# Inverse row transform by even and odd frequencies, issued in a hand-written order

## The chip, the cores and the metric

The kernel runs on one core of a Trainium2 chip. The core has a matrix engine (TensorE, PE in the profile), a vector engine (VectorE, DVE), a scalar engine (ScalarE, ACT), GpSimd (POOL) and a queue engine that only issues transfers (SyncE, SP). Times are device microseconds of one execution; a kernel's time is the median of several runs.

## What is computed

The input x has shape 16 x 16 x 256 x 256 (batch b, channel, row y, column x). Two layers follow, each of the form "add to x what a block makes of the group norm of x":

```python
# layer 0: a Laplace operator with learned poles, in the frequency domain
alpha = fft2(gn(x))
output_residue1 = einsum('biox,oxik->bkox', alpha, S)        # steady part
x1 = ifft2(output_residue1).real
x2 = einsum('kbiqz,biqx->kizx', F, E2).real                  # transient part, from the poles
x = x + x1 + x2 / Nx / Ny
# layer 1: convolutions, mish and a channel gate, on gn(x)
x = x + _L1_conv_ref(gn(x), ...)
```

gn is a group norm with 8 groups of 2 channels. Since x1 is real, the transform back needs only half of the row frequencies, 128 of them with a real and an imaginary part. The change concerns the last steps of layer 0: the inverse transform along the rows (over y), the sum with x2 and with x, the mean and variance of the result, and its normalized copy for layer 1.

## The kernel before

The program has four parts, one after the other, that hand tensors on through device memory: layer0_forward (forward transforms, pole sums, and tables that are computed in small pieces between its steps), layer0_mix (the mixing of channels and the inverse transform along the columns), layer0_back (the inverse transform along the rows and the norm) and layer1. All arithmetic is fp32.

*layer0_mix* writes hd. Its function columns (line 680 on) makes, for each row frequency fy and each half q of the batch, a tile o of 128 partitions (8 batches x 16 channels) with a real and an imaginary row of 256 columns, by a copy of the odd half on ACT (line 701) and two additions on DVE (704 and 705). One transfer per tile, issued by POOL (line 709), stores it; the real frequencies 0 and 128 share a row, so they are stored by line 715. hd has the shape frequency, batch, channel, part v, column.

*layer0_back* loops over 16 batches and, in each, over four groups of four channels: 64 groups and 256 channels. Per group it loads h (four channels of hd, 128 frequencies in the partitions, 1 MB, line 815) and x (four channels, 1 MB, line 820). For every second channel a matmul of 512 columns (828) makes pf, the pole part for two channels, which ACT copies to f (832). For each channel py gets two row halves yh, and each half takes three matmuls of 256 columns: the cosine and the sine frequencies (837, v = 0 and 1, stationary operand a slice of iy) and the pole part (840, f against e2). DVE adds py into x (843) and takes the statistics of the sum (844). After four channels two aggregates (847) follow, then group_norm_scalars (lines 30 to 54), a generator that is run to its end at once: a matmul with a matrix of 1/128 for the mean over partitions (34), small DVE operations (36 to 39), a second such matmul for the variance (42), and eight small operations of DVE with a square root on ACT (44 to 53). Last, z = (x - mean) / std is written by DVE for two channels and by POOL for the other two (854), and two transfers store it to zn (863).

The instruction order of TensorE, ACT, DVE and POOL in layer0_mix and layer1 is written out by hand (manual_schedule), and in layer0_forward that of TensorE alone. In layer0_back a scheduler of the compiler sets it. SP's order, that is the order of loads and of the stores to zn, is the scheduler's everywhere. A tile pool gives each named tile a number of buffers (bufs); a writer waits until the reader of the buffer's last content is done.

Of the kernel before, what the change touches and what calls it, by code (L numbers as in the profile page):

```python
# [10 lines left out]
F32 = mybir.dt.float32  # L11
I32 = mybir.dt.int32
AF = mybir.ActivationFunctionType
ALU = mybir.AluOpType
AX = mybir.AxisListType
PSUM = bass.MemoryType.PSUM
DRAM = bass.MemoryType.DRAM

C = 16
N = 256  # L20
G = 8
P = 128
# [34 lines left out]
def load(nc, pool, src, shape, name):  # L57
    t = pool.tile(shape, F32, tag=name, name=name)
    nc.sync.dma_start(out=t, in_=src)
    return t  # L60
# [322 lines left out]
def tables(ctx, tc, d, psum, tabs):  # L383

    nc = tc.nc
    td, avd, ed = tabs
    cp = ctx.enter_context(tc.tile_pool(name="tc", bufs=1))
# [23 lines left out]
    for k in range(C):  # L411
        e = tp.tile([P, N], F32, tag="te", name="te")
# [22 lines left out]
        for h, wt in enumerate(wts):  # L435
            for part, rhs in ((0, br), (1, e)):
                nc.tensor.matmul(
                    ps[:, h],
                    lhsT=wt[:, part].rearrange("p c i m -> p (c i m)"),
                    rhs=rhs,  # L440
                    start=part == 0,
                    stop=part == 1,
# [59 lines left out]
    for i, axis in enumerate("12"):  # L502
        pr = cp.tile([P, C], F32, name=f"epr{axis}")
        pi = cp.tile([P, C], F32, name=f"epi{axis}")
        for a in range(2):
            nc.sync.dma_start(out=pr[64 * a : 64 * a + 64], in_=d[f"p{axis}r_kp"])
            nc.sync.dma_start(out=pi[64 * a : 64 * a + 64], in_=d[f"p{axis}i_kp"])
        tr = cp.tile([P, N], F32, name=f"etr{axis}")
        nc.sync.dma_start(out=tr, in_=d["ty" if axis == "1" else "tx"].to_broadcast([P, N]))
        for k in range(0, C, 2):  # L510
            arg = tp.tile([P, 2, N], F32, tag="arg", name="arg")
            n = tp.tile([P, 2, N], F32, tag="n", name="n")
            nf, af = n.rearrange("p k x -> p (k x)"), arg.rearrange("p k x -> p (k x)")
            for j in range(2):
                nc.vector.tensor_scalar(arg[:, j], tr, pi[:, k + j : k + j + 1], None, ALU.mult)

            nc.vector.tensor_scalar(n, arg, 1.0 / TWO_PI, phase, ALU.mult, ALU.add)
            nc.vector.tensor_scalar(n, n, ROUND, ROUND, ALU.add, ALU.subtract)
            nc.vector.scalar_tensor_tensor(af, nf, -c1, af, ALU.mult, ALU.add)
            nc.vector.scalar_tensor_tensor(af, nf, -c2, af, ALU.mult, ALU.add)  # L520
            nc.vector.tensor_scalar(arg, arg, turn, None, ALU.add)
            nc.vector.tensor_scalar(arg, arg, 3.1415925, -3.1415925, ALU.min, ALU.max)
            nc.scalar.activation(n, arg, AF.Sin)
            for j in range(2):
                nc.vector.tensor_scalar(arg[:, j], tr, pr[:, k + j : k + j + 1], None, ALU.mult)
            exponential(nc, tp, af)
            if axis == "2":
                nc.vector.tensor_scalar(n, n, last, None, ALU.mult)
            nc.vector.tensor_tensor(arg, arg, n, ALU.mult)
            nc.sync.dma_start(out=ed[:, i, k : k + 2], in_=arg)  # L530
            yield

# [15 lines left out]
def layer0_mix(ctx, tc, d, al, hd, tabs):  # L548
# [133 lines left out]
    def columns(g, f, yt):  # L682
# [16 lines left out]
        for q in range(2):  # L699
            odd = hp.tile([P, 2, P], F32, tag="odd", name="odd", bufs=2)  # L700
            nc.scalar.copy(odd, ph[q][:, 1].rearrange("p (v x) -> p v x", v=2))
            o = hp.tile([P, 2, 2, P], F32, tag="h", name="h", bufs=5)
            even = ph[q][:, 0].rearrange("p (v x) -> p v x", v=2)
            nc.vector.tensor_tensor(o[:, :, 0], even, odd, ALU.add)
            nc.vector.tensor_tensor(o[:, :, 1], even, odd, ALU.subtract)  # L705
            o = o.rearrange("p v h x -> p v (h x)")
            fy = 4 * g + f
            if fy % P:
                nc.gpsimd.dma_start(  # L709
                    out=hd[fy, q:nb:2].rearrange("b k v x -> b (k v x)"),  # L710
                    in_=o.rearrange("p v x -> p (v x)"),
                )
            else:
                part = fy // P
                nc.gpsimd.dma_start(out=hd[0, q:nb:2, :, part], in_=o[:, 0])

    E = mybir.EngineType
    with tc.manual_schedule(engines={E.PE, E.Activation, E.DVE, E.Pool}):
# [60 lines left out]
def layer0_back(ctx, tc, d, hd, bd, zn, mr, ed):  # L779


    nc = tc.nc
    nb = d["x"].shape[0]
    cp = ctx.enter_context(tc.tile_pool(name="bc", bufs=1))
    iy = load(nc, cp, d["iy"], [P, 2, N], "iy")
    ones = load(nc, cp, d["ones"], [P, P], "ones")

    e1 = cp.tile([P, C, N], F32, name="e1")
    e2 = cp.tile([P, C, N], F32, name="e2")
# [1 line left out]
        for i, t in enumerate((e1, e2)):  # L791
            nc.sync.dma_start(out=t[:, k : k + 4], in_=ed[:, i, k : k + 4])

    hp = ctx.enter_context(tc.tile_pool(name="bh", bufs=3))
    fp = ctx.enter_context(tc.tile_pool(name="bf", bufs=3))
    sm = ctx.enter_context(tc.tile_pool(name="bs", bufs=2))
    psf = ctx.enter_context(tc.tile_pool(name="psf", bufs=2, space=PSUM))
    psy = ctx.enter_context(tc.tile_pool(name="psy", bufs=3, space=PSUM))
    psn = ctx.enter_context(tc.tile_pool(name="psn", bufs=1, space=PSUM))

    zero = cp.tile([nb, C * (N + 2)], F32, name="zero")
# [5 lines left out]
        for x in (0, N + 1):  # L807
            nc.gpsimd.memset(t[:, :, :, x : x + 1], 0.0)

    for b in range(nb):  # L810
        r2 = fp.tile([P, P], F32, tag="r2", name="r2")
        nc.sync.dma_start(out=r2, in_=bd[b])
        for k0 in range(0, C, 4):
            h = hp.tile([P, 4, 2, N], F32, tag="h", name="h")
            nc.sync.dma_start(
                out=h.rearrange("p k v x -> p k (v x)"),
                in_=hd[:, b, k0 : k0 + 4].rearrange("f k v x -> f k (v x)"),
            )
            x = hp.tile([P, 4, 2, N], F32, tag="x", name="x")
            nc.sync.dma_start(  # L820
                out=x.rearrange("p k h x -> p (k h) x"),
                in_=d["x"][b, k0 : k0 + 4].rearrange("k (h p) x -> p (k h) x", p=P),
            )
            st = sm.tile([P, 4, 6], F32, tag="st", name="st")
            for k in range(4):
                if k % 2 == 0:
                    pf = psf.tile([P, 2, N], F32, tag="pf", name="pf")
                    nc.tensor.matmul(  # L828
                        pf, lhsT=r2, rhs=e1[:, k0 + k : k0 + k + 2], start=True, stop=True
                    )  # L830
                    f = fp.tile([P, 2, N], F32, tag="f", name="f")
                    nc.scalar.copy(f, pf)
                py = psy.tile([P, 2, N], F32, tag="py", name="py")
                for yh in range(2):
                    ys = slice(P * yh, P * yh + P)
                    for v in range(2):
                        nc.tensor.matmul(  # L837
                            py[:, yh], lhsT=iy[:, v, ys], rhs=h[:, k, v], start=v == 0, stop=False
                        )
                    nc.tensor.matmul(  # L840
                        py[:, yh], lhsT=f[:, k % 2, ys], rhs=e2[:, k0 + k], start=False, stop=True
                    )
                nc.vector.tensor_tensor(x[:, k], py, x[:, k], ALU.add)
                nc.vector.bn_stats(st[:, k], x[:, k].rearrange("p h x -> p (h x)"))
            mv = sm.tile([P, 2, 2], F32, tag="mv", name="mv")
            for g in range(2):
                nc.vector.bn_aggr(mv[:, g], st[:, 2 * g : 2 * g + 2].rearrange("p c s -> p (c s)"))
            g0 = k0 // 2
            nm, rs = mr[:, b, g0 : g0 + 2, 0], mr[:, b, g0 : g0 + 2, 1]
            for _ in group_norm_scalars(nc, sm, psn, ones, mv, 2, nm, rs):  # L850
                pass
            z = zbuf[(4 * b + g0 // 2) % 3]
            for g, eng in ((0, nc.vector), (1, nc.gpsimd)):
                eng.tensor_scalar(
                    z[:, :, 2 * g : 2 * g + 2, 1 : N + 1],
                    x[:, 2 * g : 2 * g + 2].rearrange("p k h x -> p h k x"),
                    nm[:, g : g + 1],
                    rs[:, g : g + 1],
                    ALU.add,
                    ALU.mult,  # L860
                )
            for h in range(2):
                nc.sync.dma_start(
                    out=zn[b, 1 + P * h : 1 + P * h + P, k0 : k0 + 4].rearrange("p k x -> p (k x)"),
                    in_=z[:, h].rearrange("p k x -> p (k x)"),
                )

# [435 lines left out]
def fourier_tables():  # L1305
# [33 lines left out]
    for t in tt:  # L1339
# [5 lines left out]
        "wxa": parities(wx[..., :P]),  # L1345
        "wxn": wxn,
        "ix": ix,
        "iy": iy,
        "ones": np.full((P, P), 1.0 / P),
        "pair": np.stack([np.tile(np.eye(64), (2, 1)), -np.tile(np.eye(64), (2, 1))], axis=1),  # L1350
        "gc": np.tile(np.repeat(np.eye(G), 2, axis=0), (8, 1)),
# [8 lines left out]
        "m8": np.tile(np.repeat(np.eye(8), M, axis=0), (4, 1)),  # L1360
        "mt": mt.reshape(P, 2, 16),
        "phase": np.repeat([0.25, 0.0], 64)[:, None],
        "last": np.repeat([1.0, -1.0], 64)[:, None] / (N * N),
    }
    return {name: a.astype(np.float32) for name, a in out.items()}

# [25 lines left out]
def forward(ctx, tc, d):  # L1392
# [2 lines left out]
    keep = ctx.enter_context(tc.tile_pool(name="keep", bufs=1))  # L1395
    al = dram.tile([NF, 2, 64, nb, N], F32, name="al")
    bd = dram.tile([nb, P, P], F32, name="bd")
    hd = dram.tile([P, nb, C, 2, N], F32, name="hd")
    tabs = (
        dram.tile([P, 2, C, N], F32, name="td"),  # L1400
        dram.tile([NF, P, 384], F32, name="avd"),
# [34 lines left out]
```

## Time and profile before

The time is 7599.57 us, the median of three runs (7587.35 to 7604.02). The profiled execution took 7581.6 us.

| part, as the trace bounds it | us from the start | PE busy | DVE busy | ACT busy | POOL busy |
|---|---|---|---|---|---|
| forward, main stretch | 0 to 1300 | 1192.5 | 1073.3 | 399.8 | 528.3 |
| mix, main stretch | 1500 to 2970 | 1344.5 | 987.8 | 908.6 | 191.0 |
| back, middle 200 us | 3240 to 3440 | 199.4 | 123.5 | 21.2 | 27.7 |
| layer 1 | from 3842 | the rest of the span | | | |

The back part begins with its first row matmul at 2990.2 us and ends with the last z at 3821.8 us; layer 1's first convolution starts at 3842 us.

How to read the lines below. A group of instructions has its source line, engine and operation, output and inputs with shapes and count; behind the first bar stand its total busy time in microseconds and the mean of one in nanoseconds, and behind the second the idle time of the engine just before it, with what ended that wait. A timeline line has its start and its length in microseconds first. The chain of waits is followed back from the last instruction of a stretch: at each step to what released it, or to the instruction before it on its engine. The trace shows an fp32 matmul as two instructions.

### The profile page before, as it was taken

The numbers are of one execution on the slowest core, as the hardware profiler recorded it, in microseconds if no ns is written. First come the engines' busy times: TensorE is split into PE (matmuls) and PEld (weight loads), VectorE is DVE, ScalarE is ACT, GpSimd is POOL, SyncE is SP. The second block draws the span as 40 slices with busy tenths as digits, with TensorE's granted clock in tenths as the row PEclk, the third lists the DMA queues.
The fourth block names the chain that finished last, engine by engine and source line by source line (L and its number), as shares of the span: only waits on it lengthen the run. The fifth ranks groups of instructions, "written<-read, shape, count | busy, mean of one in ns | idle before, by whom it ended". The sixth has DMA issues, their size and how long they took to land.

```text
span 7581.6 us, 148237 instructions
## 1 busy us (share of the span) xinstructions
PE 7060.1 (93%) x58664; PEld 4076.6 (54%) x58664; DVE 4908.4 (65%) x9169; ACT 3712.2 (49%) x5659; POOL 3029.4 (40%) x4126
## 2 busy tenths in 40 slices
PE   7889999799999998999979999999999999999997
PEld 5778888566667666777733333333333333333332
DVE  8999875366666665666656666666666666666662
ACT  2223333366666664111146666666666665666662
POOL 2334444211111111111135555656555666555664
PEclk9999999899999999999989999999999999999999
DMA  3444444333333335767657788888888888888886
GB/s 97 113 115 119 119 118 111 108 97 100 100 95 96 97 97 162 251 243 250 241 151 215 228 255 254 251 265 264 244 252 256 248 267 256 249 254 254 247 266 212
DMA packets 702807, 1443.62 MB, mean 190 GB/s; under 512 B 93866, under 2 KB 520038, under 8 KB 652166
## 3 DMA queue, kind: packets, MB, share of 16 engines
q1 hardware_dynamic: 557990, 959.89, 42.3%
q0 software_dynamic: 144128, 474.25, 20.4%
q8 instruction: 468, 7.67, 0.4%
q14 instruction: 221, 1.81, 0.1%
HBM read 877.25 MB, written 556.47 MB: 189 GB/s over the span
## 4 chain that ended last, share of the span: by engine, by line
PE 67%; DVE 4%; issue 3%; ACT 3%; DMA 3%; POOL 1%; SPq 0%; DVEq 0%; POOLq 0%; ACTq 0%
PE c2ps L1111 16%; PE c L969 12%; PE pd L1037 12%; PE py L837 6%; PE ph L692 5%; PE ps L635 5%; PE pg L657 4%; PE py L840 3%; ACT wide L1017 3%; DVE alb L594 2%; PE pr L996 2%; PE pf L828 1%; DMA rows<-cf 1%; PE pt L673 1%; DMA z<-zn 1%
## 5 line engine op out<-in xcount | busy, mean ns | idle before, releaser
L1017 ACT ACTIVATE wide<-c,b 32x512 f32<-32x512 f32 x2176 | 1477.4, 679 | 353.9 <-PE c L969 302.7
L1045 DVE TENSOR_TENSOR t<-pd,r 64x512 f32<-64x512 f32 x1088 | 744.2, 684 | 1286.0 <-PE pd L1037 1263.2
L1048 DVE TENSOR_TENSOR top<-pd,t 32x512 f32<-32x512 f32 x2176 | 1503.1, 691 | 52.6
L1111 PE MATMUL c2ps<-rows,c 128*32 128x512 f32 x12288 | 1391.3, 599 | 17.8 <-ACT e L1120 15.6
L969 PE MATMUL c<-z,w 102*128 102x512 f32 x2048 | 1014.7, 628 | 135.9 <-ACT wide L1017 113.8
L1029 POOL COPY wide<-wide 32x1031 f32<-32x1031 f32 (+1 forms) x576 | 568.9, 988 | 1233.5 <-ACT wide L1017 1206.2
L1037 PE MATMUL pd<-wide,dw 128*128 128x512 f32 x2048 | 1014.4, 617 | 6.5 <-DVE top L1048 2.8
L1111 PEld LDWEIGHTS c2ps<-rows,c 128*32 128x32 f32 x12288 | 392.8, 109 | 982.3 <-issue 873.9
L969 PEld LDWEIGHTS c<-z,w 102*128 102x128 f32 x2048 | 401.1, 198 | 674.3 <-issue 485.3
L1037 PEld LDWEIGHTS pd<-wide,dw 128*128 128x128 f32 x2048 | 377.1, 194 | 614.6 <-issue 446.7
L709 POOL DMA_DIRECT2D hd<-h x254 | 188.6, 743 | 1269.3 <-DVE h L705 1249.4
L1030 POOL COPY wide<-wide 32x1031 f32<-32x1031 f32 (+1 forms) x576 | 572.2, 993 | 35.6
L1120 ACT ACTIVATE e<-c2ps,b 128x512 f32<-128x512 f32 x256 | 175.9, 687 | 834.6 <-PE c2ps L1111 831.9
L313 PE MATMUL px<-wxn,u 128*64 128x256 f32 x4224 | 558.9, 385 | 2.1 <-ACT o L320 1.8
L837 PE MATMUL py<-h,iy 128*128 128x256 f32 x2048 | 541.8, 383 | 5.2 <-DMA h<-hd 5.2
L635 PE MATMUL ps<-tt,lt 128*64 128x256 f32 x4224 | 496.5, 384 | 38.9 <-DVE lt L621 34.5
L692 PE MATMUL ph<-ix,yt 64*128 64x256 f32 x4128 | 501.6, 390 | 7.1 <-issue 6.4
L313 PEld LDWEIGHTS px<-wxn,u 128*64 128x64 f32 x4224 | 401.1, 136 | 127.5 <-ACT o L320 5.4
L837 PEld LDWEIGHTS py<-h,iy 128*128 128x128 f32 x2048 | 385.2, 191 | 108.4 <-issue 44.0
L692 PEld LDWEIGHTS ph<-ix,yt 64*128 64x128 f32 x4128 | 392.2, 189 | 93.3 <-issue 46.1
L207 PE MATMUL pu<-fy,eo 128*128 128x128 f32 x2048 | 426.0, 291 | 13.0 <-DVE u L224 8.9
L988 ACT ACTIVATE bot<-c,b 128x512 f32<-128x512 f32 x544 | 343.9, 683 | 175.2 <-PE c L969 167.3
(199 smaller groups left out, 10307.1 us busy)
## 6 DMA issues: line engine op xcount, KB each, us to landing
rows<-cf SPq DMA_DIRECT2D x128, 2176.0 KB
z<-zn SPq DMA_DIRECT2D x768, 257.8 KB
cf<-top POOLq DMA_DIRECT2D x512, 240.0 KB, 7.0
cf<-bot POOLq DMA_DIRECT2D x96, 840.0 KB, 11.5
alc<-al SPq DMA_DIRECT2D x264, 256.0 KB
zn<-zb SPq DMA_DIRECT2D x128, 516.0 KB
o<-zn SPq DMA_DIRECT2D x128, 516.0 KB
z<-in_x SPq DMA_DIRECT2D x64, 1024.0 KB
```

The lines of the kernel that those rows point to most:

```text
L313: nc.tensor.matmul(ps[64 * k : 64 * k + 64, :, h], lhsT=u[:, h, part, g0 + j + k].rearrange("p f c -> p (f c)"), rhs=wxn[:, h, part], star ...
L635: nc.tensor.matmul(ps[64 * h : 64 * h + 64, v], lhsT=lt[:, h, k, 1 - v : 3 - v].rearrange("p l f c -> p (l f c)"), rhs=tt[:, h, k], start= ...
L692: nc.tensor.matmul(ph[q][:, e], lhsT=yt[lanes, i].rearrange("p t k -> p (t k)"), rhs=ix[lanes, i], start=n == 0, stop=n == 3,)
L837: nc.tensor.matmul(py[:, yh], lhsT=iy[:, v, ys], rhs=h[:, k, v], start=v == 0, stop=False)
L969: nc.tensor.matmul(ps[:, a], lhsT=w, rhs=z[:k, c : c + 2, 0:N], start=True, stop=True)
L1017: nc.scalar.activation(self.feat[64 - 32 * q : 96 - 32 * q, f, self.groups[g], :H], ps[q][32 * f : 32 * f + 32], AF.Mish, bias=b1[0][32 * ...
L1029: nc.gpsimd.tensor_copy(flat[0:32, f, 1:m], flat[64:96, f, 0 : m - 1])
L1030: nc.gpsimd.tensor_copy(flat[96:128, f, 0 : m - 1], flat[32:64, f, 1:m])
L1037: nc.tensor.matmul(ps, lhsT=dwt if self.tail else dw, rhs=self.feat[:, f, cs, :H], start=True, stop=True,)
L1045: nc.vector.tensor_tensor(t[64:128], ps[:64], self.r[:, cs], ALU.mult)
L1048: nc.vector.tensor_tensor(self.top[32 * f : 32 * f + 32, cs, q], ps[lanes], t[lanes], ALU.add)
L1111: nc.tensor.matmul(ps[32 * j : 32 * j + 32], lhsT=c2[:, blk, dx, :], rhs=t[:, 4 * j + blk : 4 * j + blk + 4, x : x + H], start=(blk, dx) = ...
```

## The change

The inverse transform along the rows is split by the parity of the row frequency. With E(y) the sum over even and O(y) the sum over odd frequencies, for y in the first half of the rows, the row y is E + O and the row y + 128 is E - O. So hd is stored by parity: for each of the two parities its 128 partitions hold the real and the imaginary part of 64 frequencies, and one matmul per parity makes E or O for 128 rows. Only the first 128 columns of iy remain. The pole part is brought to the same form: its table e1 becomes the sum and the difference of its two row halves, made once in the table pieces of layer0_forward, with the factor 1/2 put into "last".

DVE then combines the two: ACT copies O out of PSUM, DVE writes E + O and E - O to a new tile o, and POOL adds o to x. Stores of hd become one per part v, with rows of 1 KB instead of 2 KB, and h is loaded by two transfers.

The order of issue in layer0_back is now written out by hand for TensorE, ACT, DVE and POOL: one channel per step; the matmul of the pole part runs two channels ahead; the statistics of a channel are taken one step after it; and the norm of a group is cut into four pieces (aggregates, mean, variance and scalars, z), one per step, behind the channels of the next group. There are four buffers for py instead of three, four for x instead of three, and three for the small tiles instead of two. group_norm_scalars itself is unchanged.

The core of the diff:

```diff
@@ tables
             nc.vector.tensor_tensor(arg, arg, n, ALU.mult)
+            if axis == "1":
+                lo, hi = arg[:, :, :P], arg[:, :, P:]
+                nc.vector.tensor_tensor(n[:, :, :P], lo, hi, ALU.add)
+                nc.vector.tensor_tensor(n[:, :, P:], lo, hi, ALU.subtract)
+                arg = n
             nc.sync.dma_start(out=ed[:, i, k : k + 2], in_=arg)
@@ layer0_mix, columns
-            if fy % P:
-                nc.gpsimd.dma_start(
-                    out=hd[fy, q:nb:2].rearrange("b k v x -> b (k v x)"),
-                    in_=o.rearrange("p v x -> p (v x)"),
-                )
-            else:
-                part = fy // P
-                nc.gpsimd.dma_start(out=hd[0, q:nb:2, :, part], in_=o[:, 0])
+            for v in range(2):
+                if fy % P or v == 0:
+                    part = fy // P if fy % P == 0 else v
+                    nc.gpsimd.dma_start(
+                        out=hd[fy % 2, part, fy % P // 2, q:nb:2].rearrange("b k x -> b (k x)"),
+                        in_=o[:, v],
+                    )
@@ layer0_back
-    hp = ctx.enter_context(tc.tile_pool(name="bh", bufs=3))
+    hp = ctx.enter_context(tc.tile_pool(name="bh", bufs=4))
-    sm = ctx.enter_context(tc.tile_pool(name="bs", bufs=2))
+    sm = ctx.enter_context(tc.tile_pool(name="bs", bufs=3))
-    psy = ctx.enter_context(tc.tile_pool(name="psy", bufs=3, space=PSUM))
+    psy = ctx.enter_context(tc.tile_pool(name="psy", bufs=4, space=PSUM))
-                for yh in range(2):
-                    ys = slice(P * yh, P * yh + P)
-                    for v in range(2):
-                        nc.tensor.matmul(
-                            py[:, yh], lhsT=iy[:, v, ys], rhs=h[:, k, v], start=v == 0, stop=False
-                        )
-                    nc.tensor.matmul(
-                        py[:, yh], lhsT=f[:, k % 2, ys], rhs=e2[:, k0 + k], start=False, stop=True
-                    )
-                nc.vector.tensor_tensor(x[:, k], py, x[:, k], ALU.add)
-                nc.vector.bn_stats(st[:, k], x[:, k].rearrange("p h x -> p (h x)"))
+    def fetch(i):
+        ...
+        h = hp.tile([P, 2, 4, N], F32, tag="h", name="h", bufs=3)
+        for e in range(2):
+            nc.sync.dma_start(
+                out=h[:, e].rearrange("p k x -> p (k x)"),
+                in_=hd[e, :, :, b, k0 : k0 + 4].rearrange("v f k x -> (v f) (k x)"),
+            )
+        ...
+    def channel(n):
+        ...
+        for e in range(2):
+            nc.tensor.matmul(py[:, e], lhsT=iy[:, e], rhs=h[:, e, k % 4], start=True, stop=False)
+            nc.tensor.matmul(
+                py[:, e],
+                lhsT=f[:, k % 2, P * e : P * e + P],
+                rhs=e2[:, k],
+                start=False,
+                stop=True,
+            )
+        odd = fp.tile([P, N], F32, tag="odd", name="odd")
+        nc.scalar.copy(odd, py[:, 1])
+        o = fp.tile([P, 2, N], F32, tag="o", name="o")
+        nc.vector.tensor_tensor(o[:, 0], py[:, 0], odd, ALU.add)
+        nc.vector.tensor_tensor(o[:, 1], py[:, 0], odd, ALU.subtract)
+        nc.gpsimd.tensor_tensor(x[:, k % 4], x[:, k % 4], o, ALU.add)
+    def moments(n):
+        _, x, st = groups[n // 4]
+        nc.vector.bn_stats(st[:, n % 4], x[:, n % 4].rearrange("p h x -> p (h x)"))
+    def norm(i):
+        ...
+        for g in range(2):
+            nc.vector.bn_aggr(mv[:, g], st[:, 2 * g : 2 * g + 2].rearrange("p c s -> p (c s)"))
+        yield
+        ...
+        yield from group_norm_scalars(nc, sm, psn, ones, mv, 2, nm, rs)
+        z = zbuf[i % 3]
+        for g, eng in ((0, nc.vector), (1, nc.gpsimd)):
+            eng.tensor_scalar(
+                ...
+            )
+        ...
+    with tc.manual_schedule(engines={E.PE, E.Activation, E.DVE, E.Pool}):
+        for i in range(3):
+            fetch(i)
+        rows_poles(0)
+        last = iter(())
+        for n in range(C * nb + 5):
+            if n and n % 4 == 0 and n <= C * nb:
+                fetch(n // 4 + 2)
+            if n < C * nb:
+                channel(n)
+                if n % 2 == 0:
+                    rows_poles(n + 2)
+            if 1 <= n <= C * nb:
+                moments(n - 1)
+            if n and n % 4 == 0 and n <= C * nb:
+                last = norm(n // 4 - 1)
+            next(last, None)
@@ tables of constants
-        "iy": iy,
+        "iy": iy[..., :P].reshape(64, 2, 2, P).transpose(2, 0, 1, 3).reshape(P, 2, P),
-        "last": np.repeat([1.0, -1.0], 64)[:, None] / (N * N),
+        "last": np.repeat([0.5, -0.5], 64)[:, None] / (N * N),
@@ forward
-    hd = dram.tile([P, nb, C, 2, N], F32, name="hd")
+    hd = dram.tile([2, 2, 64, nb, C, N], F32, name="hd")
```

## What I expected, before the changed kernel ran

> **What bounds the kernel now.** I read the busy shares by stretch first, to find the stage that the edit touches (the transform back along the rows, about 2990 to 3822 us), then the chain of waits inside it. One stretch of the busy shares (us, then busy us and count of PE, weight loads, DVE, ACT, POOL, granted clock, DMA share, GB/s):
>
> ```profile
> 3240.00:3440.00 200.00, 199.37 (x864) 156.31 (x863) 123.54 (x321) 21.19 (x46) 27.74 (x16) 1.00 0.69 244
> ```
>
> TensorE never pauses, at full clock; DVE is at 62%, ACT and POOL are nearly empty, DMA has room. The chain through 15 us of it (start, us, what) shows one period:
>
> ```profile
> 3305.60 0.86 PE pf L828 x2
> 3306.46 0.86 PE py L837 x4
> 3307.32 0.56 PE py L840 x2
> ...
> 3313.53 0.38 PE gn_mean L34 x2
> ...
> 3314.88 0.12 PE gn_var L42 x2
> ...
> 3318.56 0.86 PE pf L828 x2
> ```
>
> From one pf to the one two later, 3305.60 to 3318.56, is 12.96 us: one group of four channels, and there are 64 groups (829 us). The trace splits each fp32 matmul in two records, so a 256-column matmul costs 2 x 0.216 = 0.432 us and the 512-column pf 0.86. A group: 24 x 0.432 = 10.37, 2 x 0.86 = 1.73, two norm matmuls 0.50, and some 0.36 of small slips (0.56 for 0.43 after an ACT wait). Only TensorE is on this chain. The other engines, by groups of instructions in the stage (busy us, mean ns | idle before):
>
> ```profile
> L844 DVE BATCH_NORM_STATS2 st<-x 128x6 f32<-128x512 f32 x256 | 177.8, 694 | 6.6
> L843 DVE TENSOR_TENSOR x<-py,x 128x512 f32<-128x512 f32 x256 | 177.1, 692 | 237.6 <-PE py L840 235.1
> L854 POOL TENSOR_SCALAR zb<-x,mr 128x1024 f32<-128x1024 f32 x63 | 110.4, 1752 | 726.5 <-DVE mr L53 704.6 <-DMA r<-bd 11.2 <-DMA h<-hd 10.7
> L832 ACT COPY f<-pf 128x512 f32<-128x512 f32 x125 | 73.1, 585 | 615.4 <-PE pf L828 592.5 <-PE py L840 22.9
> L854 DVE TENSOR_SCALAR zb<-x,mr 128x1024 f32<-128x1024 f32 x63 | 51.2, 812 | 2.3
> ```
>
> DVE waits for TensorE, not the reverse.
>
> **What the Trainium skill says.** (1) "SBUF — State Buffer", section "SBUF: two separate sides": DVE and GpSimd share a port pair as an exclusive lock. A DVE operation with two SBUF inputs, or in a two-port mode, and a GpSimd operation shut each other out for a whole instruction. The forward stage agrees (start, us, engine, instruction):
>
> ```profile
> 764.59 2.63 POOL L194 TENSOR_TENSOR eo<-z 128x1024 f32<-128x1024 f32 x1 [4.47 <-PE pv L214]
> 766.38 0.69 DVE L174 BATCH_NORM_STATS2 st<-z 128x6 f32<-128x512 f32 x1 [1.39 <-DMA z<-in_x]
> 766.99 1.02 DVE L224 TENSOR_TENSOR u<-pu,right 128x256 f32<-128x256 f32 x2
> ...
> 785.55 2.35 POOL L194 TENSOR_TENSOR eo<-z 128x1024 f32<-128x1024 f32 x1 [2.04 <-PE pv L214]
> 785.60 2.33 DVE L51 TENSOR_TENSOR gnt<-gnt,gnv 128x2 f32<-128x2 f32 x1
> ```
>
> A two-element product from SBUF took 2.33 us, as long as the POOL instruction beside it; the statistics, and an addition with one PSUM operand, ran beside POOL at their usual cost. (2) "GPSIMD Engine Reference", "4.1 Engine selection": two-input elementwise work is about twice as slow there as on VectorE; the prices below agree. (3) "TensorE: Matmul & The Clock Gate", "Loop structure matters more than you think": idle gaps over some 3 us cost TensorE its clock; the gaps forecast here are under 1 us, so I keep 1.00. (4) "DMA: Bandwidth & Descriptors", "Specifications", gives about 358 GB/s to and from HBM per core; this trace moved 380 to 407 GB/s in several 5 us stretches from 2985 to 3020 us, so I take 380.
>
> Prices for the new work, rows of other stages (after the bar: busy us in all, mean ns of one):
>
> ```profile
> L704 DVE TENSOR_TENSOR h<-ph,odd 128x256 f32<-128x256 f32 x258 | 109.9, 426 | 316.6 <-ACT odd L701 316.6
> L705 DVE TENSOR_TENSOR h<-ph,odd 128x256 f32<-128x256 f32 x258 | 106.4, 412 | 0.0
> L701 ACT COPY odd<-ph 128x256 f32<-128x256 f32 x258 | 85.5, 383 | 49.9 <-PE ph L692 49.7
> L131 POOL TENSOR_TENSOR p<-pr 128x512 f32<-128x512 f32 x4 | 4.2, 1039 | 47.8 <-DMA pr<-in_p2r 30.3 <-DMA pr<-in_p1r 17.4
> L265 POOL TENSOR_TENSOR acc<-acc,t 128x256 f32<-128x256 f32 x48 | 34.8, 725 | 103.7 <-DVE t L252 103.7
> ```
>
> **The change part by part.**
>
> *TensorE.* Four 256-column matmuls per channel in place of six: 2 x 0.432 x 256 = 221 us less. A group is then 16 x 0.432 + 1.73 + 0.50 + 0.2 of slips = 9.35 us.
>
> *DVE.* The one 0.69 addition per channel goes; two of about 0.42 come (L704 and L705 are the same shape, one PSUM operand), starting 0.34 apart in the timeline since they don't depend on each other. Per channel 0.34 + 0.34 + about 0.61 of statistics = 1.29; four make 5.2. Per group add 0.4 for the two aggregates, 0.45 and 1.4 for the norm's scalars (the second with the 0.43 round trip to ACT's root, as at 3289.12 to 3289.55) and 0.75 for z: 8.2 us without waits.
>
> *ACT.* 4 x 0.383 + 2 x 0.585 + 0.20 = 2.9 us, hidden; but each addition now waits for the copy of the odd half, some 0.05 + 0.38 + 0.06 = 0.49 us after the last matmul. Behind the waiting addition DVE queues the statistics and the norm.
>
> *POOL.* New: x plus o, 128x512, two SBUF inputs. Between 0.725 (256) and 2.35 (1024) a line gives 0.725 + 256 x 2.12 ns = 1.27; L131, which reads one tile twice, gives 1.04. I take 1.27 and keep both ends. POOL's half of z shows 1.75, but it starts 0.13 behind DVE's 0.81 half in every group: less the 0.69 that it stood locked out, 1.06. A group of POOL: 4 x 1.27 + 1.06 = 6.1 us, hidden as a sum.
>
> *The new waits, through the fixed order.* Set t = 0 where the aggregates of a group end on DVE. TensorE, which has the next channel done, runs the mean (0.48), the second channel (1.73), a pf (0.86), the variance (0.23) and the third channel (1.73): 5.03. Odd copy: 5.52. Two additions: 6.32. POOL then adds that channel into x until 7.59, and meanwhile DVE has ended its statistics (6.9) and stands before z, a two-port operation: it waits 0.7 for POOL's port. z to 8.35; the fourth channel's additions (its matmuls were ready at 6.8) to 9.03; statistics of the third to 9.76; aggregates to 10.09; TensorE's mean 0.05 later. One period is 10.1 us: DVE's 8.2 plus the lock and the wait for the third channel. The mean waits for DVE behind one finished channel, so TensorE idles about 0.75 per group. The product before the variance also meets POOL's lock (about 0.4), but the variance is issued at 3.07 and its input is there at 2.6: no cost. The buffers that grew (py 4, x 4) are deep enough for this lag of one channel.
>
> *Transfers.* A group still moves 2.10 MB in and 1.06 MB out; at 380 GB/s that is 8.3 us, under the period. h comes as two loads with 4 KB rows instead of one with 8 KB, two groups (20 us) ahead. Hidden.
>
> *Transform along the columns before it.* Stores of hd go from 258 to 512, each half as big. On POOL that is 254 x 0.74 = 189 us more in a stretch of 1470 us where POOL is busy 191: hidden; their five buffers span two steps of some 11 us, a store lands in 5.6.
>
> *Tables.* Sixteen two-input DVE operations of about 0.41, 6.6 us, in the forward stage, where DVE is busy 1073 of 1300 us beside TensorE's 1193. I charge half of that, 3, and 3 for the end of the stage, where five more steps of the order are issued behind the last channel.
>
> Sum: 7599.6 - 64 x (12.96 - 10.1) + 6 = 7599.6 - 183 + 6 = 7423.
>
> **The rivals.** *TensorE stays the bound*: z finds the port free, or POOL takes 1.04, and DVE hides. Period 9.35, 7599.6 - 231 + 6 = 7375. For it: DVE's bare 8.2. Against: z stands right behind an addition that POOL has just begun. *POOL goes first at the lock*: when POOL's addition ends, its own half of z is next in its queue; if it starts before DVE's half, DVE waits 1.06 more. Period about 11.2, 7493. The trace has no case of both waiting at one release; DVE has stood longer, which speaks for DVE. *DVE and POOL run one after the other*: the additions lose the port to POOL as well. 8.2 + 6.1 = 14.3 us, 7599.6 + 64 x 1.34 + 6 = 7691, slower than before. Against it: L224 at 766.99 beside a POOL addition.
>
> **How the numbers follow.** The period of 10.1, 0.43; TensorE bound, 0.22; POOL first, 0.25; one after the other or some unseen cost that eats the gain, 0.10, of which 0.07 slower, 0.02 no difference. The predicted time is the likeliest case, 7423. The range from 7365 to 7515 takes in the first three with the bounds of POOL's addition and the 6 us of small costs. Faster 0.91, same 0.02, slower 0.07.
>
> **What would show it.** In the profile after: py down by a third in count; a period near 10.1; TensorE idle some 0.75 per group before the mean, released by DVE's aggregate; POOL's addition near 1.27; DVE's z showing more than 0.81 because its wait for the port counts as its own time, and POOL's z then at about 1.75 or, if POOL went first, near 1.06. The column stage and the second layer should keep their lengths. It is wrong if POOL's addition takes 2 us or more, if the odd copy arrives late behind the root on ACT, or if stores with 1 KB rows hold up the column stage.

## The result, and the profile after

The changed kernel takes 7392.98 us, the median of five runs (7375.21 to 7397.75), against 7599.57 (five runs, 7584.59 to 7606.49). The ratio is 0.9728, with a 95% interval of 0.971 to 0.9747: 207 us, or 2.7%, are gone. One run of the last kernel below took 15519 us, twice as long as its others, and is left out of that kernel's median and ratio.

First the busy shares of the transform back along the rows, by stretch (us, then busy us and count of PE, weight loads, DVE, ACT, POOL, granted clock, DMA share, GB/s):

```profile
3190.00:3390.00 200.00, 191.75 (x822) 147.93 (x821) 178.86 (x514) 59.06 (x145) 135.23 (x102) 1.00 0.95 326
```

TensorE, busy 199.37 of 200 us before, now has gaps; DVE is at 89%, POOL at 68%, and the transfers went from 0.69 to 0.95 of their time. The chain of waits in that stage (start, us, what) shows one period:

```profile
3304.72 0.38 PE gn_mean L34 x2
3305.11 0.54 PE py L858 x2
...
3306.94 0.86 PE pf L847 x2
...
3309.84 0.38 ACT odd L867
...
3310.58 0.41 DVE o L870
3311.00 0.60 DVE st L875
3311.60 1.30 DVE zb L890
3312.89 0.33 DVE o L869
3313.23 0.33 DVE o L870
3313.56 0.60 DVE st L875
3314.16 0.26 DVE mv L883 x2
3314.46 0.38 PE gn_mean L34 x2
```

From one mean to the next, 3304.72 to 3314.46, is 9.74 us where it was 12.96, and the chain now runs through three engines: TensorE for two channels, ACT for the odd half, DVE for z and the last statistics. 64 x (12.96 - 9.74) = 206 us, as much as the 207 us between the medians. Measured by its ends, from the first row matmul to DVE's last z, the stage went from 831.6 to 631.0 us, 200.6 less; the two profiled executions as wholes differ by only 190.4 us, mainly since layer 1 is 11.7 us longer in the second one (more on this under the small costs). The stage begins at 2987.9 us instead of 2990.2, so no loss in the stages ahead of it shows.

The groups of instructions in the stage (busy us, mean ns of one | idle before, releaser):

```profile
L871 POOL TENSOR_TENSOR x<-x,o 128x512 f32<-128x512 f32 x256 | 324.0, 1266 | 216.7 <-DVE o L870 215.3 <-DMA o<-zn 1.4
L875 DVE BATCH_NORM_STATS2 st<-x 128x6 f32<-128x512 f32 x256 | 175.1, 684 | 0.2 <-POOL x L871 0.2
L890 POOL TENSOR_SCALAR zb<-x,mr 128x1024 f32<-128x1024 f32 x63 | 102.8, 1632 | 0.0
L890 DVE TENSOR_SCALAR zb<-x,mr 128x1024 f32<-128x1024 f32 x63 | 86.9, 1379 | 0.0
L34 PE MATMUL gn_mean<-mv,ones 128*128 128x2 f32 x126 | 24.1, 261 | 25.1 <-DVE mv L883 25.1
```

The statistics wait 0.2 us in all for POOL's addition, although each needs one: the lag of one channel hides it. TensorE waits for DVE's aggregate, 25.1 us over 62 groups, 0.40 each. And z on DVE takes 1379 ns instead of 812. The timeline (start, us, engine) shows why:

```profile
3311.08 1.27 POOL L871 TENSOR_TENSOR x<-x,o 128x512 f32<-128x512 f32 x1 [1.55 <-DVE o L870]
3311.52 1.38 DVE L890 TENSOR_SCALAR zb<-x,mr 128x1024 f32<-128x1024 f32 x1
3312.33 1.63 POOL L890 TENSOR_SCALAR zb<-x,mr 128x1024 f32<-128x1024 f32 x1
```

DVE's z stands from 3311.52 until POOL's addition lets the port go at 3312.35, and ends at 3312.90; POOL's half of z, next in its queue, comes second and ends at 3313.96.

### The profile page after: what moved, and what is told of

The parts are those of the page before. It is cut to its first block, busy times and chain, and to the rows that moved or that the text cites. A ratio compares the mean times of both kernels' runs of the same rounds, so it can differ in the third digit from the quotient of the medians.

```text
span 7391.2 us, 147380 instructions
## 1 busy us (share of the span) xinstructions
PE 6831.1 (92%) x57640; PEld 3890.3 (53%) x57640; DVE 4961.8 (67%) x9441; ACT 3806.5 (51%) x5915; POOL 3475.6 (47%) x4636
## 4 chain that ended last, share of the span: by engine, by line
PE 64%; DVE 7%; ACT 4%; issue 3%; DMA 2%; POOL 0%; SPq 0%; DVEq 0%; ACTq 0%; POOLq 0%
PE c2ps L1169 17%; PE c L1027 12%; PE pd L1095 12%; PE ph L698 5%; PE ps L641 5%; PE pg L663 4%; ACT wide L1075 3%; DVE alb L600 2%; PE pr L1054 2%; PE py L858 2%; PE py L859 2%; PE pt L679 1%; DVE zb L890 1%; DVE st L875 1%; DMA rows<-cf 1%
## 5 line engine op out<-in xcount | busy, mean ns | idle before, releaser
L718 POOL DMA_DIRECT2D hd<-h x512 | 323.5, 639 | 1227.6 <-DVE h L711 1203.5
L320 ACT ACTIVATE o<-px,rsc 128x512 f32<-128x512 f32 (+1 forms) x272 | 186.0, 686 | 472.2 <-PE px L313 441.1
L871 POOL TENSOR_TENSOR x<-x,o 128x512 f32<-128x512 f32 x256 | 324.0, 1266 | 216.7 <-DVE o L870 215.3
```

## The experiments

The prediction's theory is a chain of latencies across engines, hidden by the order of issue except for one wait at POOL's port. The rivals that the runs can tell apart are TensorE as the plain bound, and the question which part of the change earns the time: less arithmetic, or the order.

### Each half alone

**The split without the order.** hd, tables, matmuls, additions and buffers as in the changed kernel, but the compiler's scheduler orders the stage and each norm is issued at once.

```diff
-    with tc.manual_schedule(engines={E.PE, E.Activation, E.DVE, E.Pool}):
-        ... (one channel per step, statistics a step later, norm in pieces)
+    for i in range(4 * nb):
+        fetch(i)
+        for n in range(4 * i, 4 * i + 4):
+            if n % 2 == 0:
+                rows_poles(n)
+            channel(n)
+            moments(n)
+        for _ in norm(i):
+            pass
```

> The even and odd split with the new tables, stores, loads and buffers, but the order of issue in the back part left to the compiler's scheduler and the norm of a group issued at once behind its four channels. The order that the scheduler makes puts the whole norm, from the mean to the last scalar, in one piece on DVE. Theory (the gain needs the order, because TensorE's mean and variance wait for DVE in the middle of a group): TensorE stands while DVE goes through that piece, and the last statistics of a group wait for POOL's addition of 1.27 us; the period per group is 11.3 us (10.3 to 12), so 7393 + 64 x 1.6 = about 7495 us. Rival (the split alone brings the gain, the order adds nothing): 9.74 us as in the changed kernel, 7393 us.

Measured 7607.24 us, ratio 1.0017 (1.001 to 1.0025). Both expectations missed: a third fewer row matmuls, and the kernel is a little slower. The busy shares by stretch and the waits (engine, line waited for: us in all, times, longest) of this kernel:

```profile
3190.00:3390.00 200.00, 162.62 (x596) 118.51 (x597) 123.55 (x374) 41.67 (x106) 96.44 (x75) 0.91 0.69 236
```

```profile
DVE st L875 <- POOL x L871: 146.9, 224, 1.4
...
PE gn_mean L34 <- DVE mv L883: 113.9, 63, 5.1
```

The statistics stand behind POOL's addition in 224 of 256 channels, up to 1.4 us, and what DVE owes to later channels stands behind them. TensorE waits for the aggregate 1.8 us per group, and its clock falls to 0.91. The work that was saved came back as waiting and as a lower clock.

**The order without the split.** The hand-written order, the buffers and the norm in pieces, with the six matmuls of before and DVE's one addition of py into x; tables and hd as before.

> The hand-written order and the buffers of the changed kernel, but the old arithmetic: six row matmuls per channel, DVE adding py into x, the old layout of hd. Theory (before, TensorE is the only bound of the back part): the order can remove only its small slips, 10.37 + 1.73 + 0.50 + 0.2 = 12.8 us per group instead of 12.96, about 7590 us, hardly to be told from 7600. Rival (the order itself is what speeds the part up): a period of 12.4 us or less, under 7564 us.

```diff
-        for e in range(2):
-            nc.tensor.matmul(py[:, e], lhsT=iy[:, e], rhs=h[:, e, k % 4], start=True, stop=False)
-            nc.tensor.matmul(py[:, e], lhsT=f[...], rhs=e2[:, k], start=False, stop=True)
-        ...
+        for yh in range(2):
+            for v in range(2):
+                nc.tensor.matmul(py[:, yh], lhsT=iy[:, v, ys], rhs=h[:, k % 4, v], start=v == 0, stop=False)
+            nc.tensor.matmul(py[:, yh], lhsT=f[:, k % 2, ys], rhs=e2[:, k], start=False, stop=True)
+        nc.vector.tensor_tensor(x[:, k % 4], py, x[:, k % 4], ALU.add)
```

Measured 7569.21 us, ratio 0.9968 (0.9956 to 0.9981). In the chain of waits of this kernel:

```profile
3304.73 0.12 PE gn_mean L34 x2
...
3308.40 0.12 PE gn_var L42 x2
...
3317.25 0.12 PE gn_mean L34 x2
```

The period is 12.52 us, 0.44 less than before; 64 x 0.44 = 28 us, of which the times show 23. The mean takes 0.12 instead of 0.38 because its input is long there when TensorE comes to it. Both expectations missed, by little: the theory's 12.8 us charged the norm's two matmuls with 0.50 us, which take 0.24 here, and the rival's 12.4 is not reached. TensorE is busy for all of the 200 us from 3190 to 3390 in this kernel, so there is no more waiting for an order to remove. Against the kernel before on the same chip, the split alone is 15 us slower and the order alone 23 us faster; both together are 202 us faster on another chip (the unedited kernel below). The gain belongs to neither half.

### The two parts of the order

**The statistics right behind the additions**, in the step of their own channel instead of one later.

```diff
-            if 1 <= n <= C * nb:
-                moments(n - 1)
+            if n < C * nb:
+                moments(n)
```

> The changed kernel, with one edit: the statistics of a channel are issued right behind its additions instead of one step later; the norm keeps its four pieces. Theory (with the split, x is only complete after POOL's 1.27 us, and DVE can hide that only by doing the next channel first; this is also what the scheduler's order lost): DVE stands 1.3 us per channel, 0.34 + 0.41 + 0.1 + 1.27 + 0.05 + 0.69 = 2.85 us per channel, and with 3 us of norm per group the period is about 14 us, 7393 + 64 x 4.3 = 7670 us, slower than the kernel before. Rival (the pieces of the norm alone carry the order's gain): 9.74 to 10.2 us, at most 7425 us.

Measured 7740.57 us, ratio 1.0192 (1.0161 to 1.0223): slower than before, as the theory said, and by twice what it said. The waits and the busy shares of this kernel:

```profile
DVE st L875 <- POOL x L871: 326.6, 237, 1.4
```

```profile
3190.00:3390.00 200.00, 150.08 (x528) 113.93 (x527) 103.52 (x327) 36.46 (x93) 81.05 (x65) 0.84 0.60 207
```

The expected wait is there, 1.4 us in nearly every channel, and TensorE stands 3.8 us before each mean (225.0 us over 59). What the 14 us left out is the clock, 0.84 in this stretch. In the chain the py matmul pairs behind the mean take 0.85 us and more, where they took 0.43 to 0.54 in the changed kernel:

```profile
3305.24 0.59 PE gn_mean L34 x2
3305.83 1.06 PE py L858 x2
3306.89 0.85 PE py L859 x2
...
3320.74 0.53 PE gn_mean L34 x2
```

The period is 15.5 us here, and 15.2 in every second group. This one lag is worth 350 us, against 7390.66 us for the unedited kernel on the same chip (below), the lost clock included.

**The norm in one step** instead of four, with all else as changed.

```diff
             if n and n % 4 == 0 and n <= C * nb:
-                last = norm(n // 4 - 1)
-            next(last, None)
+                for _ in norm(n // 4 - 1):
+                    pass
```

> The changed kernel, with one edit: the norm of a group is issued in one step, the one in which its aggregates are made, instead of one piece per step over four. Theory (the pieces hide the round trips between TensorE, DVE and ACT): TensorE stands about 1.3 us before the mean and 1.0 us before the variance with nothing behind them to run, the period goes from 9.74 to about 11.7 us, the time to about 7393 + 126 = 7519 us. Rival (TensorE's stalls are small beside DVE's lock and stay hidden): 9.74 us, 7393 us.

Measured 7561.08 us, ratio 0.9957 (0.9942 to 0.9972), 42 us above the theory. The chain of waits shows two unequal periods:

```profile
3303.38 0.40 PE gn_mean L34 x2
3304.40 0.38 PE gn_var L42 x2
3304.79 0.54 PE py L858 x2
...
3314.80 0.40 PE gn_mean L34 x2
...
3316.21 0.83 PE py L858 x2
3317.03 0.85 PE py L859 x2
...
3327.90 0.40 PE gn_mean L34 x2
```

The first is 11.42 us, near the 11.7 of the theory; the second is 13.10, because after its norm the py pairs take 0.85. Of the 15 periods from 3191 to 3380 us, five take 11.4 and ten 13.1. All have the same gap: 1.28 us of waiting before the mean and 0.64 before the variance, so that some 2.7 us hold nothing but two matmuls of two columns. TensorE alone in a stretch behind the second norm (us, then busy us and count of PE, granted clock, DMA share, GB/s):

```profile
3316.00:3318.00 2.00, 2.00 (x7) 0.58 0.88 354
```

**The same, with the gaps filled.** Three matmuls that nobody reads behind the mean's step and two behind the variance's, to keep TensorE busy while it waits.

```diff
-                for _ in norm(n // 4 - 1):
-                    pass
+                for step, _ in enumerate(norm(n // 4 - 1)):
+                    for _ in range((3, 2, 0, 0)[step]):
+                        nc.tensor.matmul(fill, lhsT=iy[:, 0], rhs=e2[:, 0], start=True, stop=True)
```

> The kernel with the norm in one step (7561 us, period 11.4 us where TensorE kept its clock, 13.1 where its matmuls took 0.85 instead of 0.43 us after the gap), with one edit: TensorE fills its gaps with matmuls whose result nobody reads, three of 256 columns before the mean and two before the variance, 2.2 us of work per group. Theory (the gap of some 3 us around the norm costs TensorE its clock, and this is the rest of the loss): the clock in the back part returns to 1.00, the period becomes about 11.65 us and the time falls to about 7516 us although TensorE does more. Rival (the loss is in the waits alone, the clock follows from something else): the added work lengthens the period or leaves it, 7561 us or more.

Measured 7501.8 us, ratio 0.988 (0.9861 to 0.99). Busy shares by stretch, without and with the filling:

```profile
3190.00:3390.00 200.00, 170.01 (x640) 129.40 (x640) 126.33 (x398) 45.17 (x111) 108.06 (x80) 0.91 0.73 252
```

```profile
3190.00:3390.00 200.00, 199.97 (x874) 158.67 (x875) 138.90 (x439) 49.28 (x121) 117.33 (x88) 1.00 0.79 277
```

Five more matmuls per group, 64 x 5 x 0.43 = 138 us of work on TensorE, made the kernel 59 us faster (on different chips, on which the kernel before differs by 1 us). The period is 11.48 us in nearly every group; the forecast had 11.65 and 7516 us. So of the 168 us that the norm's pieces are worth, about 59 are the clock and the rest waiting.

### The wait at POOL's port

**A longer addition in front of z.** For every fourth channel POOL's addition covers 1024 elements instead of 512. The extra half adds the fourth channel's o to the group's first channel too, so the computation is changed there.

```diff
-        nc.gpsimd.tensor_tensor(x[:, k % 4], x[:, k % 4], o, ALU.add)
+        if k % 4 == 3:
+            two = x[:, 0:4:3]
+            nc.gpsimd.tensor_tensor(two, two, o.unsqueeze(1).to_broadcast([P, 2, 2, N]), ALU.add)
+        else:
+            nc.gpsimd.tensor_tensor(x[:, k % 4], x[:, k % 4], o, ALU.add)
```

> The changed kernel, with one edit that is wrong in its output: POOL's addition for the fourth channel of each group covers 1024 elements instead of 512 (it adds o to the first channel's x once more, after that channel's statistics were taken). By the line through POOL's rows it takes 2.35 us instead of 1.27. Theory (DVE's z stands before POOL's lock until that addition ends, and this wait is on the path): z ends 1.08 us later in each group, the period goes from 9.74 to 10.8 us, the time to about 7393 + 69 = 7462 us. Rival (z's 1.38 us has another cause): 9.74 us and 7393 us, because the statistics of the fourth channel are only taken after z.

Measured 7456.42 us, ratio 0.9819 (0.9801 to 0.9837), 6 us below the theory. In the chain of waits:

```profile
3303.50 2.45 DVE zb L894
3307.51 0.38 PE gn_mean L34 x2
...
3314.39 2.45 DVE zb L894
3318.40 0.38 PE gn_mean L34 x2
```

z went from 1.30 to 2.45 in the chain, 1.15 more, and the period from 9.74 to 10.89, also 1.15 more. POOL's addition takes 2352 ns there instead of 1266, 1.09 us more, and all of it comes out in the period, so this wait is on the path.

**z out of the way of the addition.** DVE's half of z is issued ahead of a channel, at the start of its step, where no addition of POOL is running; POOL's half at the end of the step. The unedited changed kernel ran beside it, on the same chip.

```diff
         for g, eng in ((0, nc.vector), (1, nc.gpsimd)):
+            if g:
+                yield
             eng.tensor_scalar(
...
+            if n % 4 == 3:
+                next(last, None)
             if n < C * nb:
                 channel(n)
```

> The changed kernel, with one edit: DVE's half of z is issued at the beginning of its step, ahead of the channel, when POOL has nothing running; POOL's half stays at the end of the step. Theory (z waits for POOL's port): z takes 0.81 us instead of 1.38 and is off the path, but then the fourth statistics of a group must wait for POOL's addition of the third channel, which now ends at 8.55 us after the aggregates, so the period only falls from 9.74 to about 9.5 us, 7393 - 15 = 7378 us. Rival (z's length does not depend on POOL): z stays at 1.38 and the period at 9.74 or more.

> The changed kernel again, unedited, so that the other runs of this set stand beside it on the same chip: a period of 9.74 us and about 7393 us. It also shows how far the stages that the edit does not touch move between executions; the first layer-1 part was 11.7 us longer in the profile after than in the profile before.

The unedited kernel again took 7390.66 us, ratio 0.9737 (0.9722 to 0.9751). With z moved it is **7366.71 us, ratio 0.9703 (0.9687 to 0.9719)**, 24 us less and the fastest kernel of this study; the slowest of its runs, 7368.04, is below the fastest of the unedited kernel, 7387.48. A group and the busy shares of it:

```profile
L892 DVE TENSOR_SCALAR zb<-x,mr 128x1024 f32<-128x1024 f32 x64 | 52.0, 813 | 2.6 <-DVE mr L53 0.3
```

```profile
3190.00:3390.00 200.00, 200.00 (x852) 151.45 (x852) 171.67 (x533) 60.64 (x149) 132.93 (x107) 1.00 0.98 339
```

z is at its bare 813 ns, so the theory about the port is right. Its number was 11 us too high: it expected the fourth statistics of a group to wait for POOL instead, and all such waits together are 1.4 us. TensorE shows no gap any more, and the period is 9.39 us (timeline: start, us, engine):

```profile
3302.36 0.38 PE L34 MATMUL gn_mean<-mv,ones 128*128 128x2 f32 x2
...
3305.29 0.38 PE L42 MATMUL gn_var<-gnq,ones 128*128 128x2 f32 x2
...
3311.75 0.38 PE L34 MATMUL gn_mean<-mv,ones 128*128 128x2 f32 x2
```

What holds it at 9.39 was not isolated. TensorE is busy all the time, but both matmuls of the norm still take 0.38 us, as with a late input, and not the 0.12 of the kernel with the order alone. Two fewer matmuls per channel than in that kernel would leave TensorE 12.52 - 8 x 0.432 = 9.06 us, an estimate; the transfers, at 0.98 of their time, need some 9.2 (worked out below). Three limits, TensorE's own work, its inputs from DVE and the transfers, lie within about 0.3 us of one another here.

### A longer lag brings nothing more

Three kernels lengthen the lag on top of that: statistics two steps late and the norm's pieces a step later; the same with five x buffers instead of four; and that with the variance one step further behind the mean.

```diff
-            if 1 <= n <= C * nb:
-                moments(n - 1)
-            if n and n % 4 == 0 and n <= C * nb:
+            if 2 <= n <= C * nb + 1:
+                moments(n - 2)
+            if n > 1 and n % 4 == 1 and n <= C * nb + 1:
...
-        x = hp.tile([P, 4, 2, N], F32, tag="x", name="x")
+        x = hp.tile([P, 4, 2, N], F32, tag="x", name="x", bufs=5)
...
     yield
+    if late:
+        yield
     var = psum.tile([P, n], F32, tag="gn", name="gn_var")
```

> The edit of z_early, and the statistics taken two steps after their channel instead of one, with the norm's pieces one step later each. Theory (what is left above TensorE's own work is DVE waiting for POOL, once at z and once at the statistics): both waits go, TensorE stops standing before the mean, which then takes 0.12 instead of 0.38 us, and the period is 8.64 + 0.24 + 0.2 = 9.1 us by TensorE, or about 9.25 us if the transfers are full first (their share was 0.95 at 9.74 us); 7393 - 31 = 7362 us (7350 to 7375). Rival (DVE's own work or its order is the bound): 9.5 us or more.

> The kernel with statistics two steps late and DVE's half of z early (7384.7 us, 9.69 us per group), with one edit: five buffers for x instead of four. Theory (z, one step later, gave x's buffer free only when its next load was due, so the load's issue waited 3 us per group for z and the loads behind it came late): POOL no longer waits for x, and the period is 9.3 us (9.2 to 9.4), set by TensorE and by transfers that are nearly full, 7393 - 28 = 7365 us, as with z early alone. Rival (the transfers' rate or DVE is the bound): it stays at 9.69 us, 7385 us.

> The kernel with statistics two steps late and five x buffers, whose period is 9.69 us; here the variance of a group is moved one step (one channel) further behind its mean, and z a step with it. Theory: in that kernel TensorE stands before the variance's matmul in every group, 20.4 us over 59 of them, because the product of the small tile ahead of it on VectorE waits for POOL's port (0.95 us instead of 0.16) and only one channel of matmuls lies between mean and variance. With a second channel between them the wait goes: period about 9.4, time 7365, TensorE busy 199 to 200 of 200 us. Rival (the transfers at 0.95 of their time, or another wait of the longer lag such as the x loads, hold the period): 7385 as before.

Measured: 7384.66 us (ratio 0.9724, 0.9709 to 0.9738), 7386.36 (0.9731, 0.9707 to 0.9755) and 7378.38 (0.9719, 0.9696 to 0.9743). All three missed the theory, which had 7362, 7365 and 7365.

The waits of the first show what the longer lag costs: POOL stands for loads of x, 70.0 us in all. In the second kernel this wait is gone, without any effect on the time. TensorE's wait before the variance is in both:

```profile
POOL x L871 <- DMA x<-in_x: 70.0, 31, 2.3
...
PE gn_var L42 <- DVE gnq L39: 22.1, 59, 0.6
```

The chain of waits of the second names another cause:

```profile
3313.27 0.95 DVE gnq L38
3314.24 0.17 DVE gnq L39
3314.46 0.38 PE gn_var L42 x2
```

The product of the small tile meets POOL's addition at the port (0.95 us), and TensorE stands before the variance. In the third kernel that wait has gone, 1.3 us in all where it was 20.4, but TensorE waits before the mean instead, 18.7 us of which one wait is 4.5:

```profile
PE gn_mean L34 <- DVE mv L885: 18.7, 63, 4.5
```

DVE is busy 184.08 of 200 us there, and the period is 9.56 us. Each wait that was taken away let the next one show, and none of the three comes down to the 9.39 of the kernel with z moved. Whether another place for the small operations would do better with the longer lag stays open; by the estimate of 9.2 us for the transfers, at most some 0.2 us per group, 12 us in all, are left to win.

## Why the prediction was right

The forecast was 7423 us, in a range of 7365 to 7515, from a period of 10.1; measured were 7393 and 9.74.

*What bounds it before, and what leaves TensorE.* Right. The order alone, with the six matmuls, came to 12.52 with TensorE never idle. The 9.35 worked out for TensorE and the 9.39 of the kernel with z moved agree in part by luck: the 9.35 charges the norm's two matmuls with 0.50 us, one of them with a late input, where the kernel with z moved has both late, and TensorE's own work is nearer to the 9.06 estimated above.

*The chain through the engines.* Right in its links and in its first part: from the mean to the start of z the working had 6.85 us (6.9 less the 0.05 ahead of the mean), and the chain shows 3304.72 to 3311.60, 6.88. Mis-sized by 0.36 was the rest. From the start of z to its end the working took 0.7 of waiting and 0.76 of z, 1.45; measured are 1.30, since z ends 0.55 after the port is free. And from there to the next mean it took 0.68 + 0.73 + 0.33 + 0.05 = 1.79, measured 1.57 (3312.89 to 3314.46): what follows the statistics starts 0.60 behind them, not 0.73, and the aggregates cost 0.26. The 0.73 stood against the prediction's own price of about 0.61, given a few paragraphs before; with that price the period would have come to 9.97. 0.15 + 0.22 is the whole difference of 0.36 but for rounding, 64 x 0.36 = 23 us. TensorE's idle time before the mean is smaller by the same, 0.40 for 0.75.

*POOL's price.* Right: 1266 ns, where the line through the two shapes gave 1.27. The row of L131, which reads one tile twice, would have misled (1.04). POOL's half of z was priced too low, 1.06 for the 1205 ns that it takes with z moved; POOL had room, so this cost nothing.

*The lock, and who goes first.* Right. The Trainium skill, "SBUF — State Buffer", section "SBUF: two separate sides", says that whichever starts first keeps the shared pair for its whole instruction; the trace agrees with 1379 ns for z behind an addition and 813 without one. It doesn't say who follows at the release. That was the rival with 0.25: here DVE followed, in all 63 groups with an addition ahead of z. The 2.45 us of the longer addition show that the wait is on the path.

*The rivals.* The time alone doesn't decide: the changed kernel misses TensorE as the bound by 0.39 us per group (9.74 and 9.35) and the forecast by 0.36, and 7393 lies nearer to that rival's 7375 than to 7423. The chain of waits and the two experiments at POOL's port decide for the theory. The range, 150 us wide, took in three of the four cases, so that the time fell inside it says little. DVE and POOL one after the other did not happen; a time on that side came out only where the lag is missing, 7740.57, and there from the statistics' wait and the clock.

*Transfers.* Hidden, but by less than the working had it. It took 380 GB/s from short stretches and a floor of 8.3 us; the stage moved 326 GB/s at 0.95 of the engines' time, and 339 at 0.98, so, as an estimate, about 344 at all of it, and 3.16 MB / 344 GB/s = 9.2 us. The figure in the Trainium skill, "DMA: Bandwidth & Descriptors", section "Specifications", 358, was nearer for a sustained rate than my 380.

*The clock.* The changed kernel kept it, as forecast (1.00). The reason I gave, that only gaps of over some 3 us count, stands in the Trainium skill, "TensorE: Matmul & The Clock Gate", in the table of "Why this matters for your kernels" and not in the section that I named. It was too generous: in the kernel with the norm in one step, with 1.28 and 0.64 us of waiting around two tiny matmuls, the clock was lost after two norms of three. The same page, section "What's actually happening", describes a window of about 3.4 us that runs free of the program; 2.7 us of near idleness that cost the clock in some groups and not in others, with the same gap in each, would fit this, but no run here shows the window itself.

*The small costs.* The 3 us for the tables can't be told: DVE is busy 1083.1 us instead of 1073.3 in the first 1300, but the back part begins no later, and over all the profiled kernels it begins between 2980.3 and 2996.2. The 3 us for the end of the stage came, or a little more: beyond its 64 periods the stage has 631.0 - 64 x 9.74 = 7.6 us, where before it had 831.6 - 64 x 12.96 = 2.2. Layer 1 is longer by 11.7 us in the two profiles (3739.2 to 3750.9 us from its first convolution), with the same code. It takes 3740.8 us with z moved, 3751.4 in the unedited kernel again and 3748.4 with the order alone, so it moves without following the split, and is not assigned to anything.

## What to carry to other kernels

Work taken from the bounding engine by a split into sums and differences becomes a chain across engines, and here it paid only with an order that puts each link's latency behind another channel's work: either half alone moved the time by less than 0.4%, both by 2.7%. Before issuing an operation of DVE that needs the port it shares with POOL, look what POOL has been given just before; moving it by one place was worth 24 us. When TensorE waits for pieces of a norm, count the clock that it loses behind the wait too.

## What the hardware showed that was not expected

- DVE's z, waiting for POOL's addition, ended 0.55 us after that addition in every group, also behind the longer one, while it takes 0.81 by itself: as if part of its start passed in the wait.
- POOL, whose next instruction was ready when its own addition ended, did not start it before the waiting DVE instruction: 1632 ns for its z on average, against 1205 where DVE's half was not beside it.
- TensorE ran the next matmuls at half rate after 2.7 us in which it had only two two-column matmuls (granted clock 0.58 from 3316 to 3318 us), and 138 us of added matmuls took 59 us off the time.
- A two-column matmul costs 0.38 us of TensorE when its input comes late, and 0.12 when it has been there.
